# Block 3's first queries, keys and values move among block 2's last steps, and blocks 1 to 3 share one division of PSUM

## Chip, cores and metric

One core of a Trainium2 chip runs the whole program in one launch. The metric is the device time of that core in microseconds (us). Engines are named as in the profile: PE is TensorE's matmul stream (PEld its weight loads), DVE is VectorE, ACT ScalarE, POOL GpSimd, and SP SyncE, which only issues DMAs here. Everything is float32 except a few masks.

## What is computed

Four residual steps over x of 4 x 512 tokens x 128 features, regrouped into two batches of 1024 tokens:

```
x = x + attn0(layernorm(x))   # block 1: two layers of full attention, 2 heads, with an MLP each
x = x + ffn0(layernorm(x))    # block 2: two layers of windowed attention, 8 heads, with a gated MLP each
x = x + attn1(layernorm(x))   # block 3: local attention (16 heads) mixed with a latent attention
x = x + ffn1(layernorm(x))    # block 4: 64 routed experts
```

What the change touches of blocks 2 and 3, in the reference's own words:

```
q, k, v = jnp.split(h @ wqkv, 3, axis=-1)            # block 2, per layer
q = l2norm(q) * qs
k = l2norm(k) * ksc
q, k = rotary_xpos(q, k)                             # q*cos*scale + rotate_half(q)*sin*scale
...
qkv = x @ qkv_w + qkv_b                              # block 3
q, k, v = jnp.split(qkv, 3, axis=-1)
local = _local_attention(heads(q), heads(k), heads(v))
...
rq = (x @ rq_w + rq_b)                               # queries of the latent attention
```

## The kernel before

**Order by beats.** Blocks 1, 2 and 3 are each a software pipeline written out by hand. A `Pipe` holds steps that are due at a beat, and within a beat in the order of their rank; `beat()` emits them. The order of emission is the order in which each engine runs its instructions, so a step that waits holds up everything behind it on its engine. Beats are no time: an empty beat costs nothing. At the seams between blocks the scheduler may put ready instructions of the next block ahead of instructions of the last one that are not ready by its own model; within a block the order is fixed.

**Block 1** (`BlockA`, batches of 1024 tokens in 8 tiles of 128 queries). Its last steps are the MLP of the last group: `up` (L466, L469, L472, L474) fills a tile `hid`, which the matmuls of `down` (L487) read. While that runs, the first unit of block 2 is begun: `first()` of `BlockB` hands block 1 the steps `clear`, `turn`, `copy`, `queries`, `square`, `sums`, `root` and `scale` of that unit.

**Block 2** (`BlockB`, 2 layers x 2 batches x 8 tiles = 32 units, 8 beats each). A unit runs `queries` (PE L714), `square` (ACT L723), `sums` (DVE L736, L737), `root` (ACT L742, L743), `scale` (DVE L748 to L752, which writes `raw`), then on POOL the rotation: `cross` (L761, writes `t`), `straight` (L768) and `both` (L775; on DVE in the first unit). PE then turns `raw` (L807), forms scores (L822), and so on; every fourth unit is followed by its MLP (`mlp`: shift L912 to L920, norm, turn L931, up L947 with gelu L952 and product L953, down L964, add L513). The rotation needs products of the position table and the learned scales, `tables(l)` (POOL L623). For layer 0 they are made in two halves, the first half, four instructions, due at beat 0 of block 2. `prep` normalises a group of four tiles for block 2 (stats on DVE L641/L642, root on POOL L645 to L648, product on ACT L652) and turns it (`features`, PE L677 and ACT L682).

**Block 3** (`BlockC`). After the loop of block 2 the first four tiles are normalised into `c_xn` (`norm` called at L591). `prep(0, 0)` of block 3 then clears `v` (POOL L1127), adds a bias to the residual (POOL L1134), turns `c_xn` (PE L1140, ACT L1141), and forms queries, keys and latent queries (PE L1145, ACT L1146) and values (PE L1152, DVE L1157). `prep(0, 1)` normalises the next four tiles by `norm_tiles` (DVE L166/L167, POOL L168 to L173). `mask` (POOL L1222) makes the masked queries `qm`, and `score` (PE L1245 the mask, L1249 the products) starts the attention.

**Memory.** Before, blocks 1 and 2 share a PSUM pool `ps_a` (four 2 KB banks of tag `bank`, two 4 KB tiles `s0` and `s1`); blocks 3 and 4 open pools `ps_tr` (2 banks), `ps_mm` (2 banks) and, in block 3, `ps_c` (`s0`, `s1`). In SBUF, pools are opened and closed as a stack, so the tiles of a later block reuse the bytes of an earlier one, and wait until those are released. The gated products of block 4 live in 32 tiles `hid`, 19 (`REST`) of them in a pool of block 4 and the others in memory that is free by then.

Of the kernel before, what the change touches and what calls it, by code (L numbers as in the profile page):

```python
# [28 lines left out]
P = 128  # L29
D = 128  # L30
# [49 lines left out]
class K:  # L80


    def col(self, name, i=0, n=P):
        at, _ = _COLS[name]
        return self.cols[:n, at + i : at + i + 1]
# [9 lines left out]
    def big(self):  # L95
        return self.ps_big.tile([P, 512], F32, tag="big", name=self.name("big"))

    def tr(self):
# [79 lines left out]
class BlockA:  # L178
# [11 lines left out]
    def __init__(self, k, es, nxt):  # L190
        nc = k.nc
        self.k, self.nxt = k, nxt
        self.p1 = es.enter_context(k.tc.tile_pool(name="a1", bufs=1))
        self.p2 = es.enter_context(k.tc.tile_pool(name="a2", bufs=2))
        self.p3 = es.enter_context(k.tc.tile_pool(name="a3", bufs=3))
        self.pipe = Pipe()
        self.st = {}
        self.b1s = self.p1.tile([P, 8], F32, name="b1s")
        self.bks = self.p1.tile([P, 2], F32, name="bks")
        self.q, self.kk, self.v = [], [], []  # L200
        for b in range(NB):
            self.q.append(self.p1.tile([P, S], F32, name=f"q{b}"))
            self.kk.append(self.p1.tile([P, S], F32, name=f"kk{b}"))
            self.v.append(self.p1.tile([P, MT, D], F32, name=f"v{b}"))
# [25 lines left out]
    def bank(self):  # L230
        return self.k.ps_a.tile([P, 512], F32, tag="bank", bufs=4, name=self.k.name("bank"))

# [122 lines left out]
    def tile(self, l, b, qt):  # L355
# [8 lines left out]
        def score():  # L364
            assert ("ready", l, b, 1) in self.st or (l, b) == (0, 0)
            t["s"] = [k.ps_a.tile([P, S], F32, tag=f"s{h}", name=k.name("s")) for h in range(2)]
            for j in range(2):
                for h in range(2):
                    rows = slice(h * 64, (h + 1) * 64)
                    keys = slice(j * 512, (j + 1) * 512)  # L370
                    nc.tensor.matmul(  # L371
                        t["s"][h][:, keys], q[rows, qt * P : (qt + 1) * P], kk[rows, keys],
                        start=True, stop=True,
                    )
            t["nm"] = [self.small("nm", [1]) for _ in range(2)]
            for h in range(2):
                nc.vector.tensor_reduce(t["nm"][h], t["s"][h], AX.X, ALU.max, negate=True)  # L377
# [47 lines left out]
    def after(self, l, b, g, st):  # L425
# [5 lines left out]
        hT = self.p3.tile([P, 512], F32, tag="hT", name=k.name("hT"))  # L431
        hid = self.p1.tile([P, 4, 512], F32, tag="hid", name=k.name("hid"))
        last = (l, b, g) == (NL - 1, NB - 1, 1)
        eng = nc.vector if last else nc.gpsimd

        def project():
# [10 lines left out]
            for h in range(2):  # L447
                ao = self.p2.tile([P, 4, D], F32, tag="ao", name=k.name("ao"))
                nc.vector.tensor_tensor(
# [89 lines left out]
class BlockB:  # L539
# [14 lines left out]
    def first(self):  # L554

        out = self.out = {}
        out["clear"], out["turn"], out["copy"] = self.features(0, 0, 0)
        self.project(0, 0, 0, None)
        root = out["root"]
        out["root"] = lambda: (self.table(True), root())  # L560
        return out
# [14 lines left out]
    def run(self):  # L576
        pipe = self.pipe
        self.tables(0)
        for n in range(1, 4):
            pipe.later(32 * n - (26 if n == 1 else 32), lambda n=n: self.prep(0, n % 2, n // 2, 1))  # L580
        pipe.later(9, self.out["rest"], rank=9)
        pipe.later(58, lambda: self.tables(1))
        for l in range(NL):
            for j in range(2):
                for b in range(NB):
                    for m in range(j * 4, j * 4 + 4):
                        self.unit(l, b, m)
                        for _ in range(8):
                            pipe.beat()

        self.norm(self.k.xo[:, :4], self.k.c_xn, 1)  # L591
        while pipe.due:
            pipe.beat()

    def bank(self):
        return self.k.ps_a.tile([P, 512], F32, tag="bank", bufs=4, name=self.k.name("bank"))

    def two(self, tag):
        return self.k.ps_a.tile([P, 1024], F32, tag=tag, bufs=1, name=self.k.name(tag))

# [11 lines left out]
    def tables(self, l):  # L612
# [3 lines left out]
        for i, n in ((1, "b_qksr"), (0, "b_qks")):  # L616
            dst = self.p2.tile([P, MT, 2, 64], F32, tag=f"tab{i}", name=k.name("tab"))
            for j in range(2):
                for m in (slice(0, MT), ) if l else (slice(0, 4), slice(4, MT)):
                    sc = k.row(n, (l * 2 + j) * 64, 64)[:, None, :].to_broadcast([P, m.stop - m.start, 64])  # L620
                    self.pipe.later(
                        (2 if l else 5 * m.start) + 2 * j + 4 * (1 - i) if l or m.start else 0,
                        lambda dst=dst, i=i, j=j, m=m, sc=sc: nc.gpsimd.tensor_tensor(  # L623
                            dst[:, m, j, :], k.b_tab[:, m, 2 * i + j, :], sc, ALU.mult
                        ),
                        rank=3 if l or m.start else -2,
                    )
            out.append(dst)
        self.tabs[l] = out[::-1]

    def norm(self, src, dst, at):
# [72 lines left out]
    def project(self, l, b, m, later):  # L704
        k, nc, st = self.k, self.k.nc, self.st[l][b]
        first = (l, b, m) == (0, 0, 0)
        t = st.setdefault("first", {}) if first else {}

        def queries():
# [47 lines left out]
        def cross():  # L757
            t2 = t["t2"] = self.p2.tile([P, 2, 8, 64], F32, tag="t2", bufs=1, name=k.name("t2"))
            r4 = t["raw"].rearrange("p (j h) d -> p j h d", j=2)
            for a, z in ((0, 32), (32, 0)):  # L760
                nc.gpsimd.tensor_tensor(  # L761
                    t2[:, :, :, a : a + 32], r4[:, :, :, z : z + 32],
                    self.tabs[l][1][:, m, :, None, a : a + 32].to_broadcast([P, 2, 8, 32]), ALU.mult,
                )

        def straight():
            r4 = t["raw"].rearrange("p (j h) d -> p j h d", j=2)
            nc.gpsimd.tensor_tensor(  # L768
                r4, r4, self.tabs[l][0][:, m, :, None, :].to_broadcast([P, 2, 8, 64]), ALU.mult
            )  # L770
# [131 lines left out]
    def mlp(self, l, b, j, later):  # L902
# [66 lines left out]
        def add():  # L969
# [3 lines left out]
            else:  # L973
                cut = slice(b * MT + j * 4, b * MT + j * 4 + 4)
                later(1, lambda: nc.gpsimd.tensor_tensor(k.xo[:, cut], k.xo[:, cut], k.xi[:, cut], ALU.add))

        for at, rank, f in (
# [14 lines left out]
def load_c(k, w, I):  # L992
# [9 lines left out]
    nc.sync.dma_start(k.c_rout, I["L1_attn_rout_w"])  # L1002
    nc.sync.dma_start(k.c_out, I["L1_attn_out_w"])


# [6 lines left out]
class BlockC:  # L1012
# [29 lines left out]
    def run(self):  # L1042
# [21 lines left out]
        def bank():  # L1064
            for tag in turn:
                wide = self.k.ps_c.tile([P, 1024], F32, tag=tag, name=self.k.name("big"))
                yield wide[:, :512]
# [49 lines left out]
    def prep(self, b, j, beats, then=lambda: None):  # L1117
# [4 lines left out]
        if j == 0:  # L1122
            st["xT"] = self.p1.tile([P, S], F32, tag="xT", name=k.name("xT"))
            st["qT"], st["kT"] = new([P, S], "qT"), new([P, S], "kT")
# [17 lines left out]

        def linear(dst, wt, n, bias):
            ps = k.mm()
            nc.tensor.matmul(ps[:n], wt, xT[:, cut], start=True, stop=True)  # L1145
            nc.scalar.activation(dst[:, cut], ps[:n], AF.Identity, bias=bias)  # L1146

        def values():
            ps = k.mm()
            for i in range(4):  # L1150
                m = j * 4 + i
# [11 lines left out]
        def linears():  # L1163
            args = (
                (st["qT"], k.c_qkv[:, :D], P, k.col("c_bq")),
                (st["kT"], k.c_qkv[:, D : 2 * D], P, k.col("c_bk")),
                (st["rqT"], k.c_rq, 32, k.col("c_rq", 0, 32)),
            )
            return [lambda a=a: linear(*a) for a in args]

        q, kk, rq = linears()
        self.pipe.chain(
            (beats, True, features), (2, True, q), (1, True, kk), (1, True, rq),
            (1, True, lambda: (values(), st.update({("ready", j): True}), then())),
        )

# [51 lines left out]
    def score(self, b, m, ip):  # L1228
# [5 lines left out]
        for h in range(2):  # L1234
            tiles.append(k.ps_c.tile([P, 2, 2, 256], F32, tag=f"s{h}", name=k.name("s")))
            prs.append(self.p5.tile([P, 4, 256], F32, tag="pr", name=k.name("pr")))
# [378 lines left out]
class Experts:  # L1615
# [3 lines left out]

    OWN, REST = 10, 19  # L1620

# [8 lines left out]
    def new(self):  # L1630
# [7 lines left out]
        n -= self.REST  # L1638
        if n == 0:
            return k.wpool.tile(shape, F32, tag="mask_l", name=name)  # L1640
        if n == 1:
            t = k.wpool.tile([P, NROW], F32, tag="rows", name=name)
# [404 lines left out]
def tile_kernel(ctx: ExitStack, tc: tile.TileContext, I, out):  # L2047
    k = K()
    setup(k, ctx, tc, I)
    psum_ab = lambda: tc.tile_pool(name="ps_a", bufs=1, space=bass.MemoryType.PSUM)  # L2050
    with tc.tile_pool(name="wb", bufs=1) as wb, tc.tile_pool(name="b0", bufs=1) as b0, psum_ab() as k.ps_a:
        b = BlockB(k, b0)
# [11 lines left out]
    with ExitStack() as ps:  # L2064
        psum = lambda n, m: ps.enter_context(
            tc.tile_pool(name=n, bufs=m, space=bass.MemoryType.PSUM)
        )
        k.ps_tr, k.ps_mm = psum("ps_tr", 2), psum("ps_mm", 2)
        wcd = ps.enter_context(tc.tile_pool(name="wcd", bufs=1))
        load_d(k, wcd, I)  # L2070
        front = Front(k, wcd)
        ex = Experts(k, front.xT, ps.enter_context(tc.tile_pool(name="c5", bufs=5)))
        with tc.tile_pool(name="ps_c", bufs=1, space=bass.MemoryType.PSUM) as k.ps_c:
            stage_c(k, front, ex)
        with tc.tile_pool(name="ps_d", bufs=4, space=bass.MemoryType.PSUM) as k.ps_big:
# [149 lines left out]
```

## Time and profile before

| | us |
|---|---|
| median of 3 runs (lowest to highest) | 1289.01 (1288.98 to 1296.74) |
| time of the profiled execution | 1289.73 |
| its span, first to last instruction | 1287.9 |
| PE busy | 1142.3 (89%) |
| DVE busy | 867.5 (67%) |
| ACT busy | 642.8 (50%) |
| POOL busy | 478.8 (37%) |

The span is the time between the first and the last instruction of one execution; 1.83 us lie around it. Block 1 takes the span up to about 342, block 2 up to about 763, block 3 up to about 1054, and block 4 the rest. The mean granted TensorE clock is 0.970. A busy share is an average over stages with different limits: PE at 89% is nearly full in most of the span, but around 340 to 365 and 740 to 770, at the two seams that the change touches, it is not, and there other engines set the pace. A timeline line gives the start, the busy time, the engine, the line of the kernel, what it writes and reads, how many, and in brackets how long the engine sat idle before it and who ended that.

### The profile page before, as it was taken

What the parts mean: (1) busy time and instruction counts of PE and PEld (TensorE: products, weight loads), DVE (VectorE), ACT (ScalarE), POOL (GpSimd) and SP (SyncE); (2) the same over time, 40 slices, a digit from 0 to 9 for tenths busy, and PEclk for the clock granted to TensorE, in tenths of its full rate; (3) what the DMA queues carried; (4) which work ended last, traced back from release to release, by engine and by line L of the source; (5) the groups of instructions that cost most, each with busy time, mean ns of one, the idle gap of its engine ahead of it and who ended that gap; (6) DMA issues with size and microseconds to landing.
All of it is one profiled execution on the core that took longest, in us unless ns stands there. A gap on an engine that the chain in (4) does not pass through costs nothing.

```text
span 1287.9 us, 23417 instructions
## 1 busy us (share of the span) xinstructions
PE 1142.3 (89%) x9381; PEld 738.6 (57%) x9441; DVE 867.5 (67%) x1789; ACT 642.8 (50%) x1209; POOL 478.8 (37%) x556
## 2 busy tenths in 40 slices
PE   5899999999578999999989867989998978998798
PEld 3566666666345666666666634555555543343688
DVE  5566666554477776776776625556568989998763
ACT  5454545444355765665655635656766754342000
POOL 2523333232488786676786542212122210000000
PEclk9999999999899999999999988989999989999799
DMA  9000000000001100010100002000000000000000
GB/s 297 1 1 1 1 1 1 2 1 1 17 18 26 27 22 18 22 26 18 26 22 18 5 16 103 2 1 2 2 1 1 2 1 1 0 17 0 25 17 18
DMA packets 19841, 25.18 MB, mean 20 GB/s; under 512 B 2762, under 2 KB 13716, under 8 KB 19476
## 3 DMA queue, kind: packets, MB, share of 16 engines
q1 hardware_dynamic: 19076, 23.02, 6.3%
q8 instruction: 75, 1.23, 0.4%
q10 hardware_dynamic: 656, 0.66, 0.2%
q14 instruction: 34, 0.28, 0.1%
HBM read 13.32 MB, written 1.05 MB: 11 GB/s over the span
## 4 chain that ended last, share of the span: by engine, by line
PE 39%; DVE 20%; ACT 7%; issue 4%; POOL 3%; DVEq 0%; POOLq 0%; ACTq 0%
PE mm L1727 5%; PE bank L947 4%; PE big L1652 4%; PE s L714 3%; PE s L822 3%; PE s L1249 2%; PE bank L867 2%; PE tr L1286 2%; DVE nm L1254 2%; DVE r_zab L1511 2%; DVE r_zab L1512 2%; PE s L1245 2%; DVE hid L1675 2%; DVE rinv L736 2%; PE bank L964 1%
## 5 line engine op out<-in xcount | busy, mean ns | idle before, releaser
L1254 DVE TENSOR_REDUCE nm<-s 128x4 f32<-128x1024 f32 (+1 forms) x64 | 71.0, 1151 | 59.1 <-PE s L1249 59.0
L377 DVE TENSOR_REDUCE nm<-s 128x1 f32<-128x1024 f32 x64 | 75.1, 1215 | 51.7 <-PE s L371 51.7
L761 POOL TENSOR_TENSOR t<-raw,tab 128x512 f32<-128x512 f32 x64 | 79.7, 1268 | 77.1 <-DVE raw L752 73.0
L1287 ACT COPY pT<-tr 128x512 f32<-128x512 f32 x120 | 70.0, 598 | 69.5 <-PE tr L1286 69.2
L1661 ACT ACTIVATE hid<-big,cols 128x512 f32<-128x512 f32 x62 | 42.0, 687 | 75.6 <-PE big L1652 75.5
L1286 PE MATMUL tr<-ident,pr 128*128 128x128 f32 x480 | 77.6, 285 | 2.2 <-ACT pT L1287 1.8
L768 POOL TENSOR_TENSOR raw<-raw,tab 128x1024 f32<-128x1024 f32 x32 | 75.5, 2360 | 2.4
L723 ACT ACTIVATE sq<-s 128x1024 f32<-128x1024 f32 x32 | 32.8, 1025 | 85.7 <-PE s L714 85.7
L383 ACT ACTIVATE pr<-s,nm 128x1024 f32<-128x1024 f32 x64 | 71.1, 1122 | 7.7 <-DVE nm L377 7.6
L775 POOL TENSOR_TENSOR raw<-raw,t 128x1024 f32<-128x1024 f32 x31 | 73.3, 2365 | 1.7
L394 PEld LDWEIGHTS bank<-ident,pr 128*128 128x128 f32 x512 | 56.2, 141 | 30.0 <-issue 22.5
L406 PE MATMUL bank<-pT,v 128*64 128x128 f32 x1024 | 72.5, 286 | 0.7 <-DVE pT L399 0.2
L1652 PE MATMUL big<-xTd,d_gate 128*128 128x512 f32 x128 | 66.2, 609 | 7.7 <-DVE hid L1675 3.9
L1652 PE MATMUL big<-xTd,d_up 128*128 128x512 f32 x128 | 68.7, 627 | 2.3 <-DVE r_above L1891 2.3
L406 PEld LDWEIGHTS bank<-pT,v 128*64 128x64 f32 x1024 | 57.2, 141 | 22.4 <-issue 11.4
L397 ACT COPY pT<-bank 128x512 f32<-128x512 f32 x64 | 34.9, 588 | 68.2 <-PE bank L394 68.2
L1286 PEld LDWEIGHTS tr<-ident,pr 128*128 128x128 f32 x480 | 54.9, 145 | 20.8 <-issue 11.5
L371 PE MATMUL s<-kk,q 64*128 64x512 f32 x256 | 64.7, 615 | 0.6 <-ACT pr L383 0.5
L394 PE MATMUL bank<-ident,pr 128*128 128x128 f32 x512 | 65.2, 276 | 0.0
L714 PE MATMUL s<-b_wqkv,hT 128*128 128x512 f32 x128 | 63.8, 622 | 1.3 <-ACT hT L682 1.3
L1727 PEld LDWEIGHTS mm<-d_down,hid 128*128 128x128 f32 x496 | 60.4, 194 | 5.7 <-DVE xo L1758 1.9
L1727 PE MATMUL mm<-d_down,hid 128*128 128x128 f32 x496 | 61.1, 278 | 1.3 <-DVE xo L1758 1.3
(363 smaller groups left out, 2792.1 us busy)
## 6 DMA issues: line engine op xcount, KB each, us to landing
vs<-v SPq DMA_DIRECT2D x60, 130.0 KB, 2.2
b_wqkv<-in_L_ffn_wqkv_dram SPq DMA_DIRECT2D x2, 768.0 KB, 8.9
b_tab<-in_c_xpos_dram SPq DMA_DIRECT2D x1, 1024.0 KB, 8.0
d_up<-in_L_ffn_Wup_dram SPq DMA_DIRECT2D x1, 1024.0 KB, 5.8
d_gate<-in_L_ffn_Wgate_dram SPq DMA_DIRECT2D x1, 1024.0 KB, 7.5
out_dram<-xo SPq DMA_DIRECT2D x3, 256.0 KB, 2.3
rows<-in_rows_dram SPq DMA_DIRECT2D x1, 760.0 KB, 7.0
b_w<-in_L_ffn_w_dram SPq DMA_DIRECT2D x2, 341.0 KB, 7.2
```

The source lines that it names most:

```text
L377: nc.vector.tensor_reduce(t["nm"][h], t["s"][h], AX.X, ALU.max, negate=True)
L383: nc.scalar.activation(t["pr", h], t["s"][h], AF.Exp, bias=t["nm"][h], accum_out=st["sums"][:, h, qt % 4 : qt % 4 + 1],)
L394: nc.tensor.transpose(ps[:, i * P : (i + 1) * P], t["pr", h][:, at : at + P], k.ident)
L406: nc.tensor.matmul(t["u"][h * 64 : h * 64 + 64, :P], v[:, kb, h * 64 : h * 64 + 64], t["pT"][:, h, kb], start=(kb == 0), stop=(kb == MT - 1),)
L714: nc.tensor.matmul(qk[:, cut], lhsT, k.b_wqkv[:, l, cut], start=True, stop=True)
L761: nc.gpsimd.tensor_tensor(t2[:, :, :, a : a + 32], r4[:, :, :, z : z + 32], self.tabs[l][1][:, m, :, None, a : a + 32].to_broadcast([P, 2, ...
L768: nc.gpsimd.tensor_tensor(r4, r4, self.tabs[l][0][:, m, :, None, :].to_broadcast([P, 2, 8, 64]), ALU.mult)
L775: eng.tensor_tensor(flat, flat, t["t2"].rearrange("p j h d -> p (j h d)"), ALU.add)
L1254: nc.vector.tensor_reduce(nm[h], view[h], AX.X, ALU.max, negate=True)
L1286: nc.tensor.transpose(ps[:, c * P : (c + 1) * P], pr[:, c, t * P : (t + 1) * P], k.ident)
L1652: self.k.nc.tensor.matmul(ps, weights[:, rows], self.xT[:, cut], start=True, stop=True)
L1727: nc.tensor.matmul(sums[part][:, cols], hid[tp, h, c][:, e, cols], k.d_down[:, c + 8 * e, :], start=start and e == 0, stop=False,)
```

## The change

It has five parts. One: one PSUM division for blocks 1 to 3, `ps_tr` (2), `ps_mm` (2) and `ps_s` (`s0`, `s1`); `bank()` takes banks of the first two in turn. Two: the first unit of block 2 reads tables of its own (`table_of`, made on POOL in the step `clear`, during block 1), the first half of the common tables moves from beat 0 to beat 7, and the `prep` of the second batch from beat 6 to beat 10. Three: in block 1 `hid` gets a pool of its own, opened last, and `ao` shares the two buffers of `kt`. Four: the norm into `c_xn` moves ahead by 8 beats, to the start of block 2's last unit, and 31 beats after that start `first_c` turns `c_xn`, and forms the first queries, keys, latent queries and values into `s0` and `s1`, where they stay; block 3 then only moves them out of PSUM, at its beat 1. Five: `xT` of block 3 gets a pool `x0` that is open throughout, and serves one of block 4's `hid` tiles later, so `REST` is 18.

```
@@ class K
+    def bank(self):
+        self.turn = not self.turn
+        return self.tr() if self.turn else self.mm()
@@ BlockA
+        self.p4 = es.enter_context(k.tc.tile_pool(name="a4", bufs=1))
...
-        return self.k.ps_a.tile([P, 512], F32, tag="bank", bufs=4, name=self.k.name("bank"))
+        return self.k.bank()
...
-            t["s"] = [k.ps_a.tile([P, S], F32, tag=f"s{h}", name=k.name("s")) for h in range(2)]
+            t["s"] = [k.ps_s.tile([P, S], F32, tag=f"s{h}", name=k.name("s")) for h in range(2)]
...
-        hid = self.p1.tile([P, 4, 512], F32, tag="hid", name=k.name("hid"))
+        hid = self.p4.tile([P, 4, 512], F32, tag="hid", name=k.name("hid"))
...
-                ao = self.p2.tile([P, 4, D], F32, tag="ao", name=k.name("ao"))
+                ao = self.p2.tile([P, 4, D], F32, tag="kt", name=k.name("ao"))
@@ BlockB
-        out["clear"], out["turn"], out["copy"] = self.features(0, 0, 0)
+        clear, out["turn"], out["copy"] = self.features(0, 0, 0)
+        own = self.own = self.p0.tile([P, 2, 2, 64], F32, name="tab_own")
+        out["clear"] = lambda: (clear(), self.table_of(own, 0, slice(0, 1)))
...
-            pipe.later(32 * n - (26 if n == 1 else 32), lambda n=n: self.prep(0, n % 2, n // 2, 1))
+            pipe.later(32 * n - (22 if n == 1 else 32), lambda n=n: self.prep(0, n % 2, n // 2, 1))
...
                         self.unit(l, b, m)
+                        if (l, b, m) == (NL - 1, NB - 1, MT - 1):
+                            assert self.st[l][0]["done"]
+                            self.norm(self.k.xo[:, :4], self.k.c_xn, 1)
+                            pipe.later(31, lambda: first_c(self.k), rank=9)
                         for _ in range(8):
                             pipe.beat()
-        self.norm(self.k.xo[:, :4], self.k.c_xn, 1)
...
+                    at = 2 + 2 * j + 4 * (1 - i) if l else 20 + 2 * j + 4 * (1 - i) if m.start else 7
                     self.pipe.later(
-                        (2 if l else 5 * m.start) + 2 * j + 4 * (1 - i) if l or m.start else 0,
...
+    def table_of(self, dst, l, m):
+        k, nc = self.k, self.k.nc
+        for i, n in ((1, "b_qksr"), (0, "b_qks")):
+            nc.gpsimd.tensor_tensor(
+                dst[:, i], k.b_tab[:, m, 2 * i : 2 * i + 2, :].rearrange("p m j d -> p (m j) d"),
+                k.row(n, l * 128, 128).rearrange("p (j d) -> p j d", d=64), ALU.mult,
+            )
@@ project
+        tab = lambda i: self.own[:, i] if first else self.tabs[l][i][:, m]
@@ block 3
+def first_c(k):
+    nc = k.nc
+    k.c_xT = k.x0.tile([P, S], F32, tag="xT", name="c_xT")
+    ps = k.bank()
+    for i in range(4):
+        nc.tensor.transpose(ps[:, i * P : (i + 1) * P], k.c_xn[:, i, :], k.ident)
+    nc.scalar.copy(k.c_xT[:, :512], ps)
+    k.c_ps = [k.ps_s.tile([P, 1024], F32, tag=f"s{h}", name=k.name("c_ps")) for h in range(2)]
+    for at, w, n in ((0, k.c_qkv[:, :D], P), (1, k.c_qkv[:, D : 2 * D], P), (2, k.c_rq, 32)):
+        ps = k.c_ps[at // 2][:n, at % 2 * 512 : at % 2 * 512 + 512]
+        nc.tensor.matmul(ps, w, k.c_xT[:, :512], start=True, stop=True)
+    for i in range(4):
+        nc.tensor.matmul(
+            k.c_ps[1][:, 512 + i * D : 512 + (i + 1) * D], k.c_xT[:, i * P : (i + 1) * P],
+            k.c_qkv[:, 2 * D :], start=True, stop=True,
+        )
@@ BlockC.prep
+        early = (b, j) == (0, 0)
+        def linear(at, dst, wt, n, bias):
+            if early:
+                ps = k.c_ps[at // 2][:, at % 2 * 512 : at % 2 * 512 + 512]
+            else:
+                ps = k.mm()
+                nc.tensor.matmul(ps[:n], wt, xT[:, cut], start=True, stop=True)
             nc.scalar.activation(dst[:, cut], ps[:n], AF.Identity, bias=bias)
...
+        if early:
+            for f in (q, kk, last, rq):
+                self.pipe.later(beats, f)
+            return
@@ Experts
-    OWN, REST = 10, 19
+    OWN, REST = 10, 18
...
+            return k.x0.tile(shape, F32, tag="xT", name=name)
```

## The prediction

> **What bounds the kernel now.** I read the page first: PE is busy for 89% of the span, but the change works at two seams where PE starves, so the average says little. I then read the chain of waits there, the timelines of the engines it passes through, and the granted clock in short windows.
>
> At the start of block 2 the chain runs through POOL:
>
> ```profile
> 337.76 4.06 issue
> 341.85 1.50 POOL tab L623 x3
> ...
> 344.63 2.43 POOL t L761 x2
> 347.06 0.23 POOL v L574 x6
> 347.29 2.29 POOL raw L768
> ...
> 349.61 1.23 DVE raw L775
> ```
>
> The timelines of DVE and POOL show why:
>
> ```profile
> 339.56 1.23 DVE L752 TENSOR_TENSOR raw<-s,y 128x1024 f32<-128x1024 f32 x1
> 341.85 2.78 POOL L623 TENSOR_TENSOR tab<-b_tab,rows 128x256 f32<-128x256 f32 x4 [4.09 <-PE bank L487]
> 344.59 2.48 POOL L761 TENSOR_TENSOR t<-raw,tab 128x512 f32<-128x512 f32 x2
> ```
>
> `raw` is there at 340.79, but the four table products wait for L487, which reads block 1's `hid`. They share no data, only memory. The rotation starts 3.8 us late.
>
> At the end of block 2 and the start of block 3 the chain is:
>
> ```profile
> 751.01 8.42 PE bank L947 x12
> 759.52 0.76 DVE hid L953
> ...
> 760.33 1.22 POOL v L1127
> ...
> 769.35 1.01 POOL qm L1222
> 770.41 0.73 PE s L1249 x16
> ```
>
> Between 760.33 and 770.36 POOL is never idle, and block 3's first scores wait for its `qm`. PE's timeline at the same place:
>
> ```profile
> 748.51 1.63 PE L931 MATMUL bank<-ident,xs 128*128 128x128 f32 x4 [4.81 <-ACT xs L652]
> ...
> 763.76 0.63 PE L1140 MATMUL mm<-ident,c_xn 128*128 128x128 f32 x4 [0.94 <-DVE xi L513]
> ...
> 770.41 0.73 PE L1249 MATMUL s<-kT,qm 32*128 32x128 f32 x16 [0.81 <-POOL qm L1222]
> ```
>
> The early projections save PE only the work that ran from 763.76 to 769.1, and POOL finishes 0.8 us after it. The granted clock (the last figure but two of each row, 1.00 is full) tells more:
>
> ```profile
> 744.00:748.40 4.40, 0.00 (x0) 0.00 (x0) 1.55 (x8) 0.54 (x3) 2.17 (x5) 0.82 0.00 0
> 748.40:749.50 1.10, 0.98 (x3) 0.54 (x3) 0.00 (x0) 1.10 (x4) 0.75 (x1) 0.50 0.00 0
> ...
> 755.00:757.00 2.00, 2.00 (x3) 0.68 (x2) 0.65 (x1) 0.46 (x1) 0.00 (x0) 0.50 0.00 0
> 757.00:759.00 2.00, 2.00 (x6) 0.79 (x5) 0.75 (x1) 0.63 (x2) 0.00 (x0) 0.99 0.00 0
> ```
>
> PE idles from 743.7. A mean of 0.82 over 4.4 us is 1.6 us at half clock, so it fell at about 746.8, after 3.1 us of idleness, and came back at about 757, after six busy us. L947 runs at half speed.
>
> **The change part by part.** Times are those of the profiled execution, whose span is 1287.9 and whose own time is 1289.73, 0.72 above the median.
>
> *PSUM, shared buffers, memory: 0.* Four banks in turn remain four banks, so each is reused at the same distance; the 0.94 us before L1140, a wait for the old pool's release, goes with L1140 itself. `ao` and `kt` share buffers: in one typical group `ao` is written at 106.44 and read by POOL until 109.83, `kt` is written at 111.79 and read until 116.4, and the next `ao` comes at 143.21. The cover is 2 us; gone, it would cost up to 2 us in each of four groups. Block 4 still has 32 tiles for `hid`. No DMA moves on a queue; SP's weight loads wait for the bias product L975 (ended 768.95) as before and come earlier with it.
>
> *Own tables.* Two products of 128x128 on POOL in block 1: L623 takes 0.70 us for twice the elements, so under 1.4 us together, inside POOL's 4.88 us of idleness before 326.34. Free. If that cover were gone, 1.4 us would delay a norm.
>
> *Start of block 2.* The tables leave the front of `cross`, and `hid` moves behind the memory that `t` takes. `cross` can start at 340.85. If `t` still waited for L487, at 341.85, 1 us less. Then by the rows: `cross` and the memsets 2.74, `straight` 2.38, so DVE's L775 starts at 345.9 for 349.61. DVE then runs L775 (1.2), the second unit's sums (1.4), the delayed stats (1.6), and scale (1.8): its `raw` ends at 352.1 for 357.3. POOL has behind `straight` the four tables (2.8), the residual L500 (1.3), a memset (0.3), the norm's root behind the stats (1.8, to 352.1) and a memset (0.5): `cross` of the second unit at 352.6 for 357.38, 4.8 us earlier. Its `both` ends at 359.9. The third unit gains more: before, its L714 ran at half clock (3.08 for 1.98), and the turn and copies of the second batch (L677, L682) stood before its L723, at 363.61; with `prep` four beats later they stand behind it. L714 can start at 352.1, L723 at 354.2, 9.4 earlier, and now POOL limits: behind `both` it has 1.2 us of copy and table, so `cross` of the third unit starts at 361.2 for 368.62, 7.4 earlier. From there the pipeline runs in units of 10.7 us that depend only on each other. The bounds are 3.7 (only the first rotation moves) and 9.4 (PE's and ACT's gain alone). I take 7.0, nearest to the third unit's POOL row. What is late next is POOL.
>
> *The earlier norm of `c_xn`: +1.6.* Its stats now fall on the same beat as those of an MLP, behind them on DVE and ahead of the last unit's sums:
>
> ```profile
> 711.76 0.18 DVE L642 BATCH_NORM_AGGREGATE ln_mv<-ln_st 128x2 f32<-128x6 f32 x1
> 711.86 1.19 DVE L736 TENSOR_REDUCE rinv<-sq 128x16 f32<-128x1024 f32 x1
> ```
>
> DVE has no gap there; eight stats took 710.27 to 711.86. POOL waits for the `raw` that follows (1.64 us idle before L761 at 715.95), and PE's L807 at 723.38 waits for POOL, so 1.59 us pass through. POOL's four root operations (1.9 us) fit in that idleness. At the old place, 720.06, DVE then idled for 1.57, so nothing comes back. Bounds 0 and 1.9.
>
> *`first_c` in the gap: -3.0.* The turn (0.6), ACT's copy (0.6 with its start) and 4.0 us of matmuls (765.11 to 769.1 before) fill PE from 743.7 to 749.0; L931, which needs the last product of L652 at 749.6, ends at 749.9 for 750.14. With no gap of 3 us the clock should hold: the twelve L947 at 0.48 (four took 1.91 at full clock elsewhere) end at 756.5, and the last L953 at 757.3 for 760.27. Bounds: 0 if the clock falls all the same, 4.0 if all 8.4 us halve.
>
> *Start of block 3.* POOL's clearing of `v` follows that L953 and its chain of 9.0 us is unchanged, so `qm` also comes 3.0 earlier, no more: the moved projections bring nothing of themselves. But PE now has only L1245 (0.6 us) between L964's end at 759.9 and `qm` at 767.4. A gap of 3.1 us dropped the clock above, so I expect half clock from 767.4 on: of the 7 us of PE work to 778.1, what falls within 3 to 6 us runs at half speed. I charge 2.0; bounds 0, and 5.0, half of the 10 us that the clock stayed low above.
>
> The Trainium skill (TensorE: Matmul & The Clock Gate, section "Why this matters for your kernels") warns of PE gaps over about 3 us between bursts, which speaks against the new gap here. In its Part 1 it gives some 3.4 us of sustained work to recover; by that estimate the charge would be 1.7 and the sum 0.3 lower. The row at 751 to 757 shows about six.
>
> Sum: -7.0 + 1.6 - 3.0 + 2.0 = -6.4, a profiled time of 1283.3, or 1282.6 against the median.
>
> **Rivals.** *A, only the first rotation's 3.7 us survive*, because DVE's long L737 (0.17 to 2.09 us, as the rows at 365.92 and 374.51 have it) or the moved tables eat the rest: -3.7 + 1.6 - 3.0 + 2.0 = -3.1, 1285.9. For it: POOL carries the same work. Against: the half-clock L714 and the copies before L723 are gone.
>
> *B, slower: the clock at block 3's start stays low.* PE works there in bursts. From 770 to 784 it was busy 11.7 us at clock 1.00; all at half speed that is 11.7 us more, less 2.3 us of idleness it can fill: 9.3 in place of 2.0, in all +0.9, 1289.9. It decides from 8.4 us, the sum of the other terms. Against: the low stretch at 747 to 757 ended after six busy us.
>
> *C, the stats hide and the clock holds*: -7.0 - 3.0 = -10.0, 1279.0. For it: free-running PE gaps may be broken by L1245. Against: DVE's row shows no gap.
>
> *D, nothing of it reaches the end*, since blocks 3 and 4 depend on clock phases of their own: 1289.
>
> **How the numbers follow.** Forecast 0.45, A 0.20, C 0.18, B 0.12, D 0.05. The likeliest is 1282.6. C with both upper bounds (9.4 at block 2's start, 4.0 from the clock) gives 1275.6, B 1289.9; the range 1275 to 1290 takes these in. One per cent, 12.9 us, is about what a measurement can tell from no change. Faster than 1276.1 needs C's best: 0.07. Slower than 1301.9 has no mechanism here: 0.03. Within: 0.90.
>
> **What would show it.** `cross` of the first unit about 1 us after `raw`, and not behind L623. The third unit's L761 some 7 us earlier. L736 of the last unit 1.6 us further behind its MLP's stats. L947 in the last MLP near 5.9 us and clock 1.00 there. At block 3, L1249 released by POOL's `qm` after a long PE gap, and a clock of 0.50 behind it. The prediction is wrong if the first tables still gate `cross`, if block 3's first scores come more than 3 us earlier against the last L953, or if clock rows later in blocks 3 and 4 differ by more than the seams do.

## The result and the profile after

| | before | after |
|---|---|---|
| median (lowest to highest), 11 runs each | 1291.11 (1288.48 to 1296.74) | 1298.62 (1296.53 to 1304.5) |
| profiled execution: time, span | 1289.73, 1287.9 | 1296.8, 1295.0 |
| mean granted clock | 0.970 | 0.971 |

The changed kernel is slower: ratio 1.0051, interval 1.0033 to 1.0069, some 7 us. The forecast was 1282.6, 6.4 us less than before, and its range ended at 1290.

To see where the time went, each instruction of DVE and ACT is matched with its counterpart in the kernel before, and the difference of their starts (median over a stretch, in us) is set against the place in the span of the kernel before. This is worked out from the two timelines; the experiments told below are in it too:

```
place in the span of before:      305   415   505   602   697   743   758   825  1005  1264
after                            -0.1  -5.3  -1.9   0.9   3.6   8.1   5.0   7.3   7.4   7.1
before, PSUM divided (e1)        -0.3   0.2   3.5   6.3   9.0  10.2  10.2  10.2  10.2  10.1
after, four banks in one tag(e2) -0.5  -5.7  -5.7  -5.6  -5.6  -4.1  -7.2  -9.7 -22.4 -24.4
after, first qm earlier (e6)     -0.7  -5.2  -1.9   0.8   3.5   6.4   3.3   2.9   1.9   2.6
before, start of block 2 (e10)    3.0  -2.1  -2.1  -2.1  -2.1  -0.7  -1.7  -0.3  -2.5  -2.9
```

A row that falls wins time there, a row that rises loses it. After wins 5.2 at the start of block 2 and 3.1 in its last MLP, loses 2.3 at the start of block 3, as the prediction's terms had it in sign and roughly in size. What the prediction did not have is the climb from -5.3 to 3.6 between 415 and 697, in six steps of 1.4 to 1.8, one at each of the first six MLPs of block 2 (a seventh stands in the climb to 8.1).

The start of block 2, in the chain of waits of the kernel after (start, length, what):

```profile
339.37 1.24 DVE raw L775
...
340.77 0.04 POOL t L784
...
342.00 1.26 POOL t L784
...
343.50 2.29 POOL raw L791
345.79 3.73 POOL tab L636 x4
...
353.47 2.46 POOL t L784 x2
```

The rotation follows `raw` at once (`t` is two products; the first starts at 340.77, the second at 342.00), and the tables, four products in 3.73 us, stand behind it. Where the rest of the expected gain stayed is seen two units on, in the timelines of POOL and DVE of the kernel after:

```profile
358.44 2.35 POOL L798 TENSOR_TENSOR raw<-raw,t 128x1024 f32<-128x1024 f32 x1
358.93 1.90 DVE L771 TENSOR_TENSOR e<-y 128x16 f32<-128x16 f32 x1 [0.53 <-ACT y L766]
360.87 0.30 DVE L772 SCALAR_TENSOR_TENSOR e<-e,rinv 128x16 f32<-128x16 f32 x1
361.20 0.66 DVE L773 SCALAR_TENSOR_TENSOR y<-e,y 128x16 f32<-128x16 f32 x1
...
363.33 2.48 POOL L784 TENSOR_TENSOR t<-raw,tab 128x512 f32<-128x512 f32 x2 [1.36 <-DVE sums L895]
```

Three DVE operations on 16 elements, 0.17 to 0.18 us each in the same unit before, take 2.86 here, and the third unit's `t` starts at 363.33: 5.3 earlier than before (368.62), not 7.4. The first of them ends at 360.83, just after POOL's L798 at 360.79. The Trainium skill (SBUF — State Buffer, "SBUF: two separate sides") describes a pair of ports that VectorE and GpSimd take from each other for a whole instruction, by a VectorE operation with two SBUF inputs among others; L771 is one, and the row agrees with it, though no run here isolated it.

Now the climb. PE's timeline at the first MLP of block 2, of the kernel before:

```profile
431.62 0.66 PE L807 MATMUL bank<-ident,raw 128*128 128x128 f32 x4 [0.34 <-ACT pT L861]
432.12 1.98 PE L947 MATMUL bank<-h,b_w 128*128 128x512 f32 x4
```

and of the kernel after:

```profile
426.46 0.66 PE L830 MATMUL mm<-ident,raw 128*128 128x128 f32 x4 [0.35 <-ACT pT L884]
427.92 1.12 PE L970 MATMUL mm<-h,b_w 128*128 128x512 f32 x2 [0.81 <-ACT kT L832]
428.89 1.02 PE L970 MATMUL tr<-h,b_w 128*128 128x512 f32 x2
...
430.82 1.12 PE L970 MATMUL tr<-h,b_w 128*128 128x512 f32 x2 [0.29 <-DVE hid L976]
```

Before, the up projection runs directly behind L807. After, its first matmul waits 0.81 us for the copy `kT` to read a bank of the pair `mm`, although the copy `pT` (ended 426.9) had freed one of the pair `tr`; the next up waits 0.29 for `hid`. Over all MLPs the groups of PE tell the same (after the bar: busy, mean ns, idle before and who ended it). Before:

```profile
L947 PE MATMUL bank<-h,b_w 128*128 128x512 f32 x64 | 34.3, 665 | 0.9 <-ACT h L933 0.9
```

After:

```profile
L970 PE MATMUL mm<-h,b_w 128*128 128x512 f32 x32 | 17.1, 615 | 3.7 <-ACT kT L832 1.6 <-DVE hid L976 1.2 <-ACT h L956 0.9
L970 PE MATMUL tr<-h,b_w 128*128 128x512 f32 x32 | 17.1, 615 | 5.0 <-ACT kT L832 3.2 <-DVE hid L976 1.8
```

8.7 us of idleness (3.7 + 5.0) for 0.9, and all that is new, 7.8, is ended by a reader of a bank, ACT's `kT` or DVE's `hid`.

The last MLP and the start of block 3, PE and POOL of the kernel after:

```profile
768.56 0.38 PE L1297 MATMUL s<-mask_c,identb 128*128 128x256 bf16 x2 [0.55 <-ACT rqT L1194]
...
772.62 2.04 POOL L1274 TENSOR_TENSOR qm<-qT,small_c 128x512 f32<-128x512 f32 x2
773.72 1.24 PE L1301 MATMUL s<-kT,qm 32*128 32x128 f32 x16 [4.78 <-POOL qm L1274]
```

and the granted clock in short windows of the same (last figure but two):

```profile
756.50:764.00 7.50, 6.52 (x21) 3.00 (x20) 1.50 (x2) 5.09 (x9) 0.75 (x1) 1.00 0.00 0
...
768.00:772.00 4.00, 0.39 (x3) 0.10 (x1) 0.51 (x1) 0.51 (x1) 3.66 (x8) 0.90 0.00 0
772.00:776.00 4.00, 2.28 (x20) 1.66 (x20) 1.01 (x2) 0.00 (x0) 4.00 (x5) 0.50 0.02 4
776.00:780.00 4.00, 3.33 (x5) 1.33 (x5) 0.97 (x2) 2.84 (x7) 1.33 (x3) 0.50 0.65 211
780.00:784.00 4.00, 4.00 (x31) 2.09 (x30) 1.88 (x3) 1.62 (x3) 0.00 (x0) 0.82 0.99 411
```

The last MLP now runs at full clock; PE then idles 4.78 us for `qm`, and the first scores of block 3 (the 16 matmuls L1301 take 1.24 for 0.73 before) run at half clock. The clock is back at about 781.4 (a mean of 0.82 over 4 us is 1.4 us at half clock), after some seven busy us.

### The profile page after: what moved, and what is told of

Read it like the earlier page. It is cut to its first block, busy times and chain, and to the rows that moved or that the text cites. A ratio compares the mean times of both kernels' runs of the same rounds, so it can differ in the third digit from the quotient of the medians.

```text
span 1295.0 us, 23445 instructions
## 1 busy us (share of the span) xinstructions
PE 1155.3 (89%) x9441; PEld 739.3 (57%) x9441; DVE 864.7 (67%) x1789; ACT 642.3 (50%) x1209; POOL 479.6 (37%) x558
## 4 chain that ended last, share of the span: by engine, by line
PE 55%; DVE 24%; ACT 11%; POOL 5%; issue 4%; DMA 0%; DVEq 0%; POOLq 0%; ACTq 0%
PE mm L1781 5%; PE big L1706 4%; PE s L379 4%; PE s L737 3%; PE s L845 3%; PE s L1301 2%; PE tr L1338 2%; PE tr L414 2%; PE s L1297 2%; PE mm L414 2%; DVE nm L385 2%; DVE nm L1306 2%; DVE r_zab L1563 2%; PE tr L970 2%; DVE r_zab L1564 2%
## 5 line engine op out<-in xcount | busy, mean ns | idle before, releaser
L798 POOL TENSOR_TENSOR raw<-raw,t 128x1024 f32<-128x1024 f32 x31 | 73.3, 2365 | 1.7
L1310 ACT ACTIVATE pr<-s,nm 128x256 f32<-128x256 f32 (+1 forms) x160 | 61.1, 470 | 2.0 <-DVE nm L1306 1.5
L851 DVE TENSOR_REDUCE nm<-s 128x8 f32<-128x1024 f32 x32 | 39.2, 1225 | 27.9 <-PE s L845 27.9
L1564 DVE TENSOR_TENSOR r_zab<-r_zab 128x128 f32<-128x128 f32 (+2 forms) x140 | 55.2, 394 | 0.0
L1563 DVE TENSOR_TENSOR r_zab<-r_zab 128x128 f32<-128x128 f32 (+2 forms) x140 | 53.6, 383 | 2.5
L1349 PE MATMUL mm<-pT,v 128*32 128x128 f32 x960 | 51.6, 289 | 0.0
```

The costliest lines, as they stand in the source:

```text
L798: eng.tensor_tensor(flat, flat, t["t2"].rearrange("p j h d -> p (j h d)"), ALU.add)
L1563: nc.vector.tensor_tensor(d[:, :, 0, :], s[:, :, 0, :], far, ALU.max)
L1564: nc.vector.tensor_tensor(d[:, :, 1, :], s[:, :, 0, :], far, ALU.min)
```

## The experiments

The theory after the result, T1: the division of the four banks into two pairs that are taken in strict turn makes matmuls of block 2's MLP wait. Rivals: T2, the moved tables, the moved norm or the shared SBUF buffers slow block 2; T3, the early norm and projections do.

**e1, the kernel before with the division alone.**

```
...
+    def bank(self):
+        self.turn = not self.turn
+        return self.tr() if self.turn else self.mm()
...
-        return self.k.ps_a.tile([P, 512], F32, tag="bank", bufs=4, ...)
+        return self.k.bank()
...
-    with ..., psum_ab() as k.ps_a:
+    with ..., psum("ps_tr0", 2) as k.ps_tr, psum("ps_mm0", 2) as k.ps_mm, psum("ps_a", 1) as k.ps_a:
```

> The kernel before, with the division of PSUM alone: blocks 1 and 2 take their four single banks from two pools of two in strict turn, as the changed kernel does, instead of from one tag of four; nothing else is changed. Theory T1 (the division makes the matmuls of block 2's MLP wait for a bank): block 2 loses about 1.4 us at each of its seven or eight MLPs, so the time is 9 to 12 us above the kernel before, about 1300 to 1303 us, and the idle time ahead of the up projections grows from 0.9 us to 7 or more. Rival T2 (the loss comes from the moved tables, the moved norm of x, or the shared buffers in SBUF): no difference, 1291 +- 2. Rival T3 (the early norm and projections of block 3 cost it): no difference either.

1300.56 us, ratio 1.0077 (1.0063 to 1.0092). In the table it climbs by 10.0 from 415 to 743, in seven steps, and then no more. The groups of PE for the up projections of e1:

```profile
L954 PE MATMUL tr<-h,b_w 128*128 128x512 f32 x32 | 19.0, 679 | 5.9 <-ACT kT L816 3.2 <-DVE hid L960 1.8 <-ACT h L940 0.9
L954 PE MATMUL mm<-h,b_w 128*128 128x512 f32 x32 | 18.2, 652 | 2.8 <-ACT kT L816 1.6 <-DVE hid L960 1.2
```

The waits of after are here with the same releasers, and nothing else of the change is in this kernel. T2 and T3 fall as explanations of the climb.

**e2, the changed kernel with one tag of four banks**, in blocks 1 to 4:

```
     def bank(self):
-        return self.tr() if self.turn else self.mm()
+        return self.ps_tr.tile([P, 512], F32, tag="bank", ...)
...
-        return self.ps_mm.tile([P, 512], F32, tag="mm", ...)
+        return self.ps_tr.tile([P, 512], F32, tag="bank", ...)
...
-    k.ps_tr, k.ps_mm = (ctx.enter_context(psum(n, 2)) for n in ("ps_tr", "ps_mm"))
+    k.ps_tr = ctx.enter_context(psum("ps_tr", 4))
```

(`tr()` likewise.)

> The changed kernel with one tag of four banks in place of the two pools of two; block 3 takes its banks from the same tag. T1: block 2 no longer loses, so at block 2's end the kernel stands 3 to 5 us ahead of the kernel before instead of 5 to 8 behind, and the whole is 9 to 12 us under the changed kernel, 1287 to 1290 us, if block 3 does not mind its pairs being joined (unknown, +-3). T2 and T3: about the changed kernel's 1298.6, +-3.

1269.3 us, ratio 0.9837 (0.982 to 0.9854): 29 us under the changed kernel. The climb is gone (-5.7 at 415, -5.6 at 697), and the group of the up projections, here of e2, waits as before:

```profile
L970 PE MATMUL bank<-h,b_w 128*128 128x512 f32 x64 | 31.4, 615 | 0.9 <-ACT h L956 0.9
```

Up to block 2's end this is T1's prediction (-4.1 at 743, expected -3 to -5). Not expected were the further 17 us in blocks 3 and 4, worked out from the medians (the profiled run, 1265.29, is the fastest of its five, so its row in the table says more); e8 takes them up.

**e3, the changed kernel with the two banks of each up in the other order.**

```
-            ag = (self.bank(), self.bank())
+            ag = (self.bank(), self.bank())[::-1]
```

> The changed kernel with the two banks of each up projection in the other order, so that the matmul written first takes the bank of the pair that is free first. T1 says that a bank freed late stands in front of a matmul while another is free: the first up of each MLP then starts without its wait, the second still waits, so between a third and all of the loss comes back, 3 to 10 us under the changed kernel: 1289 to 1296. T2 and T3: no difference, 1298.6 +- 2.

1293.8 us, ratio 1.0026 (1.0014 to 1.0037), 4.8 under the changed kernel. The groups of PE:

```profile
L970 PE MATMUL tr<-h,b_w 128*128 128x512 f32 x32 | 17.5, 628 | 0.9 <-ACT h L956 0.9
L970 PE MATMUL mm<-h,b_w 128*128 128x512 f32 x32 | 17.3, 621 | 0.0
```

The waits of the up projections are gone, by the order of two names alone, and between 415 and 697 the shift rises by 1.5 (from -4.6 to -3.1) instead of 8.9. So most of the loss in block 2 is these waits, and not others that the pairs make. The whole wins less than that: the profiled run lost some 4 us against after in block 3, with the clock at 0.66 in its window from 990 to 1000 us. The mean granted clock of the twelve runs is 0.963 to 0.968, of the eleven of the changed kernel 0.966 to 0.971; why it is lower is open.

**e4, the changed kernel without the early projections** (block 3 makes them itself; the early norm stays):

```
-                            pipe.later(31, lambda: first_c(self.k), rank=9)
...
-        early = (b, j) == (0, 0)
+        early = False
```

> The changed kernel without the early transposes and projections of block 3 (block 3 makes them itself, as before; the norm of its input stays early). My account of the clock: the last MLP of block 2 falls to half clock again and loses 3 us; the start of block 3 keeps its clock and wins 2.4 us; the sum is +0.7, 1298 to 1300. T3 (the early projections are what costs block 2): 5 to 8 us under the changed kernel, 1291 to 1294. T1 says that block 2 up to 740 us is as in the changed kernel.

1302.37 us, ratio 1.009 (1.0075 to 1.0105): 3.8 over the changed kernel, so T3 falls once more, but the time is also above the 1298 to 1300 that the account of the clock gave. Its last MLP lost the 3.0 us as expected. The start of block 3 did not win 2.4 but lost another 1.5: POOL reaches `qm` 9.0 us after it clears `v`, for 7.3 in the changed kernel, since a residual addition (L997) and two clears now stand in front of it.

**e5, the changed kernel with the norm of block 3's input later.**

```
-                            self.norm(self.k.xo[:, :4], self.k.c_xn, 1)
+                            self.norm(self.k.xo[:, :4], self.k.c_xn, 20)
```

> The changed kernel with the norm of block 3's input 19 beats later, still ahead of the early transposes. The prediction's +1.6 for the statistics that stand among block 2's last vector work: 1.6 us under the changed kernel, about 1297. Rival (the step of the timeline at 720 to 735 us is a fall of the granted clock in that one profiled run, 0.50 at 727 to 729 us, not the statistics): no difference, 1298.6 +- 1.

1297.57 us, ratio 1.0041 (1.0027 to 1.0056), not to be told from the changed kernel. Its timeline shows why: against e6, which has the early norm, it is 1.6 ahead from 715 us on, and gives back 1.15 at 745, where the statistics now stand (the rest of that comparison is a fall of the clock in this profile). So the statistics cost their 1.6 where the change put them, but at the later place most of that is paid again.

**e6, the changed kernel with block 3's first masked queries ahead of the second half's norm.**

```
...
+        for _ in range(2):
+            pipe.beat()
+        self.mask(*tiles[0])
-        self.prep(0, 1, 9, latent)
+        self.prep(0, 1, 7, latent)
         while pipe.now < 8:
             pipe.beat()
-        self.mask(*tiles[0])
```

> The changed kernel with block 3's first masked queries (POOL) issued ahead of the norm of the second half instead of behind it. In the changed kernel these queries were ready from 766.8 us on, but POOL came to them at 772.62, and the first scores waited 4.78 us for them, at half clock afterwards. Theory (the start of block 3 is now set by POOL's order, and the +2.4 us lost there come from that wait and the clock that falls in it): 4 to 7 us under the changed kernel, 1292 to 1295, and the granted clock at block 3's start stays above 0.9. Rival (what follows is bound by the second half's norm, which comes 2 us later): 0 to +2.

1295.06 us, ratio 1.0016 (1.0002 to 1.0031): 0.35% under the changed kernel. PE and POOL of e6:

```profile
766.03 1.04 POOL L1276 TENSOR_TENSOR qm<-qT,small_c 128x512 f32<-128x512 f32 x1
...
767.12 0.73 PE L1303 MATMUL s<-kT,qm 32*128 32x128 f32 x16 [0.23 <-POOL qm L1276]
...
771.04 1.33 PE L1185 MATMUL mm<-ident,xn 128*128 128x128 f32 x3 [3.19 <-POOL xn L180]
```

Counted from the last product of `hid`, the first scores come 4.9 us earlier, and at full clock, but the next wait for POOL, of 3.2 us, stands right behind them, and the clock falls there instead (0.53 from 770 to 774): the expected clock above 0.9 was wrong. From 758 to 825 the shift falls by 0.4 where after's rises by 2.3, so 2.7 of the 4 to 7 is the seam's; the other 1.6 of this profile's lead came at 727, by the clock alone (last section).

**e7, the changed kernel with six unread matmuls in that gap.**

```
+            if (b, m, ip) == (0, 0, 0):
+                fill = k.tr()
+                for _ in range(6):
+                    nc.tensor.matmul(fill, k.ident, st["xT"][:, :512], start=True, stop=True)
```

> The changed kernel with six matmuls of 512 columns, whose result nobody reads, between block 3's first mask matmuls and its first scores, where TensorE otherwise waits 4.78 us for POOL. Clock theory: the granted clock at 770 to 790 us, 0.74 in the changed kernel, rises to 0.95 or more, and the start of block 3 wins 2 to 3 us: 1296. Rival (the wait for POOL alone sets the start): no difference, or +1.

1294.42 us, ratio 1.0014 (1.0001 to 1.0027). Windows of e7 over the gap and behind it:

```profile
771.00:775.00 4.00, 4.00 (x13) 1.57 (x16) 0.00 (x0) 0.00 (x0) 3.92 (x6) 1.00 0.00 0
775.00:781.00 6.00, 5.32 (x50) 2.90 (x46) 3.09 (x5) 3.93 (x9) 3.11 (x5) 1.00 0.49 161
```

The clock holds, and the seam wins 2.4 against after (its shift goes from 5.7 to 5.6 where after's goes from 5.0 to 7.3), as expected. The wait for POOL is as before and only the idle time is filled, so the +2.3 at block 3's start is the half clock that followed that idle time; in e6, which shortens the wait without filling it, the fall comes at the wait that is left.

**e8, the kernel before with the single banks of blocks 3 and 4 in one tag of four**; blocks 1 and 2 untouched:

```
-        return self.ps_mm.tile([P, 512], F32, tag="mm", ...)
+        return self.ps_tr.tile([P, 512], F32, tag="bank", ...)
...
-        k.ps_tr, k.ps_mm = psum("ps_tr", 2), psum("ps_mm", 2)
+        k.ps_tr = psum("ps_tr", 4)
```

> The kernel before, with blocks 3 and 4 taking their four single banks from one tag of four instead of two pools of two; blocks 1 and 2 as they are. With four banks in one tag the changed kernel won 12 us up to block 2's end and 19 us behind it. If that second part is the joined banks alone: 15 to 20 us under the kernel before, 1271 to 1276. Rival (the early projections and the joined banks need each other): less than 5 us, 1286 or more.

1270.27 us, ratio 0.9825 (0.9803 to 0.9847): 23 us under its own kernel before (1293.18 in these runs). The waits of PE in block 3, of the kernel before (in all, times, longest):

```profile
PE mm L1202 <- DVE local L1319: 2.2, 1, 2.2
...
PE mm L1313 <- DVE prl L1353: 2.1, 3, 0.8
PE mm L1140 <- DVE prl L1353: 1.6, 1, 1.6
...
PE mm L1313 <- ACT latT L1385: 1.0, 1, 1.0
PE mm L1367 <- ACT qT L1146: 0.9, 1, 0.9
```

Without the entry "issue", the list comes to some 16 us there and to some 8 in e8, where none of these five is left and the longest is `PE tr L1286`, 2.3 in three waits for ACT's `pT`. So the old division of block 3 into pairs had the same fault, and the change brought it into block 2. These 8 us are not all of the 23. The longest of the waits, L1202's, ends at 856.06 in the kernel before, and its clock is at half from 856.0 to 866.2; in e8, without this wait, the clock stays at 1.00 there, and matched as in the table above it gains 6 us between the places 855 and 865. So a short wait for a bank can cost more than its length, by the clock behind it; that it set off this fall is likely from the place, but no run isolates it.

**The last four** add parts up. e9 has the edits of e2 and e6 together:

> The changed kernel with one tag of four banks everywhere and block 3's first masked queries ahead of the second half's norm: the two largest gains together. If they add up (0.9837 of the kernel before, and 0.35% less): 0.980, about 1265 us. If the joined banks already take the wait away: 0.984.

1263.86 us, ratio 0.9801 (0.9784 to 0.9818): the fastest, 27 us under the kernel before and 35 under the changed one. The two add up, within their intervals.

e10 is the changed kernel with the PSUM pools of before, and without the early norm and projections:

```
     def bank(self):
-        return self.tr() if self.turn else self.mm()
+        return self.ps_s.tile([P, 512], F32, tag="bank", bufs=4, ...)
...
-                            self.norm(self.k.xo[:, :4], self.k.c_xn, 1)
-                            pipe.later(31, lambda: first_c(self.k), rank=9)
...
+        self.norm(self.k.xo[:, :4], self.k.c_xn, 1)
```

> The kernel before with the start of block 2 as changed: own tables for the first unit, the moved tables and prep, the shared and the new buffers in SBUF; the four banks in one tag in blocks 1 and 2, the pairs in block 3, and block 3's projections as before. The prediction's sum for this part was -7.0; the changed kernel's timeline shows -5.2 from 400 us on. If nothing of it is given back in block 2: 5 to 7 us under the kernel before, ratio 0.995 to 0.996. Rival (it is given back by the end of block 2, and the shared buffers cost what the start wins): 0.999 to 1.001.

1286.92 us, ratio 0.997 (0.9956 to 0.9985), 4 us under the kernel before: somewhat less than was expected, and better than the rival. In the table (it enters block 2 at 3.0, most of it from one step near 50 us, where its clock is at half for 6.8 us) it falls by 5.1 at the start and keeps it through block 2; so the moved tables, the moved `prep` and the shared buffers cost nothing later in that block. The 1.4 at 743 are a fall of the clock in this profile (0.78 from 718 to 722, where before's has 1.00).

e11 has the edits of e2 and e7 together:

> The changed kernel with one tag of four banks everywhere and the six unread matmuls ahead of block 3's first scores. If the kept clock is worth here what it was with the pairs (0.37%): 0.980. If block 3 with four banks is bound elsewhere at its start: 0.984.

1270.33 us, ratio 0.9835 (0.9822 to 0.9848): the same as e2, so with four banks in one tag the kept clock is worth nothing to the whole. Its clock holds at the seam (1.00 from 757 to 772), but falls later, 0.54 from 780 to 790.

e12 is e10 with e8's edit for blocks 3 and 4:

> The same as the one with block 2's start alone, and blocks 3 and 4 with one tag of four banks. If the two are independent, 0.9825 and a further 0.4 to 0.5%: 0.978. Against the changed kernel with four banks (0.9837) it shows what the early projections of block 3 are worth: by the changed kernel's timeline they win 3.1 in the last MLP and lose 1.6 in the statistics and 2.4 at block 3's start, so that leaving them out costs -0.9 us, nothing that this can tell.

1267.87 us, ratio 0.9821 (0.9808 to 0.9834): the two are not independent as far as this can tell: against e8 (0.9825) the start's 0.3% no longer shows, and 0.978 is outside the interval. Leaving out the early projections costs nothing that shows against e2, as expected.

## Why the prediction was wrong, step by step

- *"PSUM, shared buffers, memory: 0. Four banks in turn remain four banks, so each is reused at the same distance."* This is the step that failed, and it decides the sign. The count of banks is the same and the distance in calls is too, but not the freedom: with one tag, a tile got a bank whose reader was done (L947 without a wait), with pairs in turn it must take one of two, and those were held by the copy `kT` and the product `hid`. (Which single bank a tile got is not in the trace; this is read from the waits and from e3.) Measured by e1: 10.0 us by the timeline, +0.77% (0.63 to 0.92) by time; by e3 and e2, it goes with the order or with the tag. The trace of before holds what a check would need: which reader frees a bank, and when, is in ACT's and DVE's rows around L947, and the new sequence of calls can be laid beside it. That this would have given the 1.4 us of each MLP was not tried. With this term, -6.4 becomes +3.6.
- *The shared buffers `ao` and `kt`, own tables: 0.* Right: block 1 ends 0.1 ahead of before, and e10 loses nothing in block 2.
- *Start of block 2, -7.0 (3.7 to 9.4).* Right mechanism, -5.2 measured, -5.1 in e10. The first rotation (340.77 for the forecast 340.85) and `both` (345.82 for 345.9) are as worked out; the second unit is 0.8 late, since the four tables took 3.73 for 2.8, and the third 2.1, of which 0.8 are the second's and 1.36 POOL's wait behind DVE, whose three small operations took 2.86. Rival A had named such long DVE rows, as the reason for a smaller gain.
- *The earlier norm, +1.6.* Right: 1.5 in e2 and e6 at 715.
- *`first_c` in the gap, -3.0.* Right: -3.1, clock 1.00 in the last MLP, and e4 loses 3.0 without it. It is no luck of one run: in the eight profiles with `first_c` the clock is full there, in the six without it falls.
- *Start of block 3, +2.0 (0 to 5).* Right: +2.3, with the idle gap and the half clock where they were expected; e7 removes it.
- *Rivals.* B had the sign, and that by luck, not the cause: the clock came back after some seven busy us. None of the rivals named a bank. That a new wait could come from the memory of PSUM needed a rival of its own, with bounds, below and above nothing; it had been given none.

The sum of the terms as measured is -5.2 + 10.2 (six steps of 8.9 in all, and 1.3 at the seventh MLP) + 1.5 + 1.6 (the clock at 727) - 3.1 + 2.3 - 0.2, 7.1: what the two profiles differ by. The 1.6 at 727 are luck of this profile, as the last section shows.

## What to carry to other kernels

Count for each buffer which reader frees it and when, not how many there are: four interchangeable banks and two pairs in turn are not the same memory. The cheapest repairs here were the order in which two tiles are asked for (e3) and one tag for both uses (e2, e8). And work moved into a PE gap can leave a new gap behind it, with a fall of the clock of its own: here that took back 2.3 of 3.1 us. Filling the new gap won them back in e7; in e11 it won nothing for the whole.

## What the runs showed of the hardware beyond that

The Trainium skill (Perfetto Trace Analysis, "Matmuls") advises to rotate independent matmul groups through different PSUM banks, so that one is read while the next is written. Both kernels do, so the advice does not tell them apart; e1, which rotates more strictly than before, took 10 us more.

A fall of the clock does not follow from the length of the gap alone. In the changed kernel's profile PE idles 2.67 us before L883 at 726.82, and the clock is at half behind it:

```profile
724.00:727.00 3.00, 0.33 (x3) 0.19 (x2) 1.64 (x2) 1.29 (x2) 2.92 (x2) 0.97 0.00 0
727.00:729.00 2.00, 2.00 (x10) 2.00 (x10) 0.00 (x0) 1.69 (x4) 2.00 (x3) 0.50 0.00 0
```

In e4 the same 2.67 us at the same place leave it at full:

```profile
729.00:732.00 3.00, 0.38 (x4) 0.14 (x2) 1.87 (x2) 1.17 (x3) 2.92 (x2) 1.00 0.00 0
732.00:734.00 2.00, 1.95 (x18) 1.95 (x19) 0.00 (x0) 2.00 (x4) 2.00 (x3) 1.00 0.00 0
```

What differs is how the gap lies in time. In each of the fourteen profiles all falls of the clock start on one grid of 3.41 us, placed differently from run to run, and each stretch at half clock lasts a whole number of its steps (3.4, 6.8, 10.2 or 13.7 us; only a last one, cut off by the end of the record, can be shorter). The gap of 2.67 us stands in all fourteen. In five of them (after, e3, e5, e10, e12) one step of the grid holds 2.24 to 2.67 us of it, and the clock is at half from the end of that step; in the other nine no step holds more than 1.97, and the clock stays. The low stretches at the last MLP of before (746.8 to 757.1) and at block 3's start of after (771.2 to 781.4) are both three steps, 10.24 us. PE is busy for some 7 us of the one in after, and in before for 7.7 rather than the six of the prediction, which left out L931.

The step at 727 is worth 1.6 us, and such steps come and go from run to run; e4's profile is 4.5 us late by 305, where nothing differs from after, some 2.3 of it by two of them (near 50 and 80 us). A term of the size of one of them is read from several timelines, not from one.
